# Cross-attention and FFN on one core: rows turned by TensorE in place of DMA transposes, the last output projection made by rows, and a new written order of all steps

## The chip, the cores and the metric

The kernel runs on one core of a Trainium2 chip. The metric is the device time of one execution in microseconds (us), lower is better. The runs shown are executions of the same program; one further execution was taken with the hardware profiler.

## The reference, cut to what matters

Eight elements of 112 tokens with 512 channels attend to contexts of 375 rows with 256 channels, in 16 heads of 128 channels; then an FFN of 512 x 2048 x 512 whose operands are rounded to 127 levels a side, by rows for the tokens and over the whole matrix for the weights.

```python
def attn(h, c):                       # h = layernorm(x)
    q = rmsnorm((h @ Wq).reshape(B, Sq, H, D), gq)
    k = rmsnorm((c @ Wk).reshape(B, Skv, H, D), gk)
    v = (c @ Wv).reshape(B, Skv, H, D)
    p = softmax(einsum('bqhd,bkhd->bhqk', q, k) / sqrt(D))
    return einsum('bhqk,bkhd->bqhd', p, v).reshape(B, Sq, H * D) @ Wo

def ffn(x):                           # x = layernorm(x)
    X1_q, sX1 = quantize_rowwise(x)   # round(x * 127 / absmax of the row), and absmax
    W1_q, sW1 = quantize_global(W1)
    X2 = gelu(X1_q @ W1_q.T * (sX1 * sW1 / 127**2) + B1)
    X2_q, sX2 = quantize_rowwise(X2)
    W2_q, sW2 = quantize_global(W2)
    return X2_q @ W2_q.T * (sX2 * sW2 / 127**2) + B2

x = x + attn(layernorm(x), ctx)
x = x + ffn(layernorm(x))
```

## The kernel before, in words

**Tiling.** Elements go in four pairs p = 0 to 3 (`BP` = 2, `NPAIR` = 4, `TP` = 224 tokens of a pair), heads in four groups of four (`HG`, `NG`). A group of a pair has a number G = 4p + g (0 to 15, `NGG` = 16), and a group of one element a number u = 2G + i (0 to 31). Attention matmuls are fp32; each shows as two matmul instructions in the profile, while transposes show as one. The FFN matmuls are bf16, for the rounded values are whole numbers to 127.

**Spare rows.** A tile has 128 rows and an element 112 tokens. The 16 spare rows of elements 1 to 7 carry element 0 (for the queries, element 7) in seven parts, so the FFN runs over seven elements, 1 to 7.

**Steps.** Each piece of work is a small function registered as a step with a short name; a word such as `w0.26` in the written order plays step `w0` at place 26. The order is written by hand as four scripts, one for each pair; negative places reach back into the pair before. TensorE, VectorE, ScalarE and the SP queue each run their instructions strictly in that order (`in_written_order`). `after(...)` only asserts that a step was played earlier; semaphores follow from the data and the buffers. All plain DMAs are issued from SP.

**Steps of attention for one u or G.** `k0..k2` keys (`pkk`), `kc`, `kq`, `kr`, `ka..kd`, `kn` their normalization, `kt`, `ks`, `kf` the turning of keys by 32x32 blocks on VectorE and two trips through DRAM (`kz`, `kd`, `kT`); `Q`, `S`, `qt`, `qs`, `qf`, `G` the same for queries; `s0..s3` scores (`sc`); `x`, `e`, `iv`, `n` softmax; `z`, `ps`, `pf` the turning of probabilities (`pz`, `pd`, `pT`), for the first and the last u by TensorE instead (`pt`, `pk`); `w0`, `w1` the probabilities times the context (`pu`, kept by `v` as `wc`); `o`, `u` times Wv (`po`, kept as `oT`); `p`, `a` times Wo (`pw`), with channels on partitions, added on VectorE into `aT`. For the last group, G = 15, `O`, `U`, `P`, `A` do this for each element alone.

**From attention to FFN.** Pairs 0 to 2: `rz`, `rs`, `rf`, `rn` turn `aT` back to rows by blocks and DRAM and add it to the tokens (`x2`). The last pair: `ra` turns `aT` on TensorE (L965) after the last `A`, and `rb` adds it. Then `st` (statistics), `fa`, `fb`, `fc`, `fd` (the root), `fi` (normalize and row maximum), `fq` (round to bf16 `xq`).

**FFN of one element.** The rows must be turned before each of the two products. Elements 6 and 7: `ti` on TensorE (L1052), kept by `tj` (L1060, VectorE); hidden rows by `tp0..tp3`, kept by `tk0..tk3` (L1060, ScalarE or VectorE). Elements 1 to 5: one DMA transpose each, `td` for the input rows and `te` for the hidden ones (`send_rows`, L1073). `h0..h3` is the first product (L1080), `i0..i3` scale and bias (L1089), `ge` (or `g0..g3`) gelu with a load of the activation table before and after, `lm` (or `mx`, `es`) the row maximum, `qh` (or `qp`, `qq`) rounding, `y0`, `y1` (or `Y0..Y3`) the second product (L1159), `yo`, `yd` the residual and the output.

**PSUM.** All matmul tiles but the scores rotate through four buffers (`mm_tile`, pool `ps_mm`): a new tile waits until the one four before has been read. Scores have four of their own.

Of the kernel before, what the change touches and what calls it, by code (L numbers as in the profile page):

```python
# [30 lines left out]
def xattn_ffn_kernel(  # L31
# [870 lines left out]
    def project(G, lo, n, c0):  # L902
        if n == TP:
            after(("u0", G), ("u1", G))
        else:
            after((f"U{lo // S}", G))
        pw = T["pw", G, lo, c0] = mm_tile(f"pw_{G}_{c0}_{lo}")
        for c in range(c0, c0 + NW // n):
            for h in range(HG):
                nc.tensor.matmul(  # L910
                    pw[:, (c - c0) * n : (c - c0 + 1) * n], T["wo", G][:, h, c * P : (c + 1) * P],
                    T["oT", G][:, h, lo : lo + n], start=(h == 0), stop=(h == HG - 1),
                )
# [13 lines left out]

    for n in range(2):
        step(f"o{n}", NG, values, 0, TP, 2 * n)
        step(f"u{n}", NG, value_keep, 0, TP, 2 * n)  # L930
        step(f"p{n}", NG, project, 0, TP, 2 * n)
        step(f"a{n}", NG, project_add, 0, TP, 2 * n)
        step(f"O{n}", NG, values, n * S, S, 0)
        step(f"U{n}", NG, value_keep, n * S, S, 0)
        step(f"P{n}", NG, project, n * S, S, 0)
        step(f"A{n}", NG, project_add, n * S, S, 0)
# [19 lines left out]
    def turn_sum(b):  # L956

        p, i = divmod(b, BP)
        if p == NPAIR - 1:
            after((f"A{i}", NGG - 1))  # L960
        else:
            after(("a0", p * NG + NG - 1), ("a1", p * NG + NG - 1))
# [50 lines left out]
    def stats(b):  # L1013
        after(("rb" if b >= B - BP else "rn", b), ("zf", b))
# [4 lines left out]
    def row_absmax(src, name):  # L1019
        m = small.tile([P, 1], F32, tag="rowmax", name=name)  # L1020
# [8 lines left out]
    def norm_in(b):  # L1029
        after(("fd", b))  # L1030
        xn = T["xn2", b] = ffn.tile([P, C], F32, tag="y", name=f"xn2_{b}")
        nc.vector.tensor_scalar(xn, x2_of(b), T["mv2", b][:, 0:1], T["rstd2", b], ALU.subtract, ALU.mult)
        T["m1", b] = row_absmax(xn, f"m1_{b}")
        T["d1", b] = dequant_scale(T["m1", b], absw1, f"d1_{b}")
# [6 lines left out]
    def quantize_in(b):  # L1041
        quantize_rows(home("xq", b, [P, C], BF16), T["xn2", b], quant_scale(T["m1", b], P))
# [27 lines left out]
    def send_rows(b, what):  # L1070

        to = home(what + "T", b, [P, KC if what == "xq" else KF, P], BF16)
        nc.sync.dma_start_transpose(out=to, in_=T[what, b])  # L1073

# [9 lines left out]
    def hidden_keep(b, n):  # L1084
        after(("lb", 0))
# [27 lines left out]
    def pieces_scale(b):  # L1113
        after(*[(f"mx{n}", b) for n in range(NF4)])
        m = small.tile([P, 1], F32, tag="rowmax", name=f"m2_{b}")
# [23 lines left out]
    def turn_piece(b, n):  # L1139
        after((f"qq{n}", b))  # L1140
# [46 lines left out]
    step("fi", BP, norm_in)  # L1187
    step("fq", BP, quantize_in)
# [3 lines left out]
    step("td", BP, send_rows, "xq")  # L1192
    step("te", BP, send_rows, "hq")
# [13 lines left out]
    for n in range(2):  # L1207
# [7 lines left out]
        cz.0 lk.0 cz.1 lf.0 lf.1 lx.0 l7.0 gl.0 lc.1 kh.0 jl.0 lk.1 lq.0 jl.3 jl.6 kh.1 xs.1 xs.0 xa.1  # L1215
        xc.1 xs.7 ct0.0 kc0.0 xa.0 xb.7 k0.1 kc1.0 xb.1 xd.1 xc.0 xm.1 xa.7 kq0.0 xc.7 k1.1 kr0.0 kq1.0
        kc2.0 xb.0 xd.0 kc0.1 kr1.0 ck0.0 ct0.1 xm.0 kq2.0 xt.1 xd.7 kc1.1 cz.2 xt.0 kr2.0 ck0.1 k2.1
        kb.0 ka.0 xm.7 ke.0 kq0.1 kd.0 xk.0 kn2.0 xt.7 xk.1 gm.0 kn0.0 kv2.0 xk.7 jm.0 kc2.1 xl.0 kv0.0
        kq1.1 lq.1 k0.2 kw0.0 kw2.0 kn1.0 xy.0 xy.1 kr0.1 kv1.0 kr1.1 kq2.1 Q0.0 kr2.1 kb.1 ka.1 jm.3
        kc0.2 ke.1 Q1.0 qt0.0 kw1.0 qs0.0 lx.1 kd.1 jl.1 kn1.1 qv0.0 kn0.1 S0.0 kt0.1 k1.2 kq0.2 kn2.1  # L1220
        S1.0 kt2.1 qw0.0 sa.0 sb.0 kc1.2 kt1.1 k2.2 kq1.2 ks.1 qt1.0 sc.0 qx0.0 sd.0 qv1.0 kr0.2 kc2.2
        k0.3 kr1.2 kq2.2 qs1.0 kr2.2 lc.2 s2.0 lv.0 kb.2 s7.0 ct1.0 qw1.0 lk.2 s1.0 qx1.0 ck1.0 s3.0
        jm.1 kc0.3 s0.0 ka.2 kq0.3 k1.3 ke.2 x0.0 kf.1 k2.3 kc1.3 ly.0 x1.0 e0.0 jl.7 Q0.1 kd.2 e2.0
        kn2.2 e3.0 kn0.2 e1.0 iv.0 xs.3 n0.0 kc2.3 kn1.2 pt0.0 n2.0 k0.4 qt0.1 S0.1 xs.2 qs0.1 n3.0
        kt0.2 kq1.3 pt2.0 pt3.0 pk0.0 kt1.2 n1.0 s1.1 kt2.2 pk2.0 ct1.1 cb0.2 kc0.4 ks.2 s0.1 cb1.2
        pt1.0 kr0.3 s3.1 kr1.3 kq0.4 k1.4 xa.3 pk3.0 jl.2 ck1.1 kr0.4 kq2.3 pk1.0 k2.4 x0.1 xb.3 s2.1
        e0.1 kr2.3 Q1.1 kc1.4 kb.3 ka.3 kc2.4 ke.3 kq1.4 kd.3 kq2.4 kn0.3 xc.3 kf.2 e1.1 x1.1 qf0.1 k0.5
        lq.2 kt0.3 lk.3 e2.1 kn2.3 e3.1 w0.0 xd.3 iv.1 kr1.4 n0.1 n2.1 z0.1 xa.2 qt1.1 w1.0 n1.1 n3.1
        kn1.3 qs1.1 S1.1 z1.1 z3.1 k1.5 z2.1 sb.1 G0.1 xm.3 ps.1 v0.0 kt1.3 s1.2 kr2.4 s2.2 kb.4 ka.4
        kt2.3 ke.4 s0.2 sa.1 xc.2 ks.3 sc.1 s3.2 kc0.5 sd.1 kc1.5 x0.2 k2.5 kq0.5 x1.2 e0.2 lo.0 Q0.2  # L1230
        kq1.5 kr0.5 kc2.5 e3.2 kd.4 kn0.4 kq2.5 e2.2 kn1.4 v1.0 qt0.2 S0.2 k0.6 pf.1 qf1.1 e1.2 cs.2
        Q1.2 kt0.4 qs0.2 kn2.4 kt2.4 iv.2 k1.6 kt1.4 n1.2 kf.3 n0.2 kr1.5 ks.4 n3.2 xb.2 z0.2 S1.2 xd.2
        jm.2 kc0.6 n2.2 lq.3 w0.1 xm.2 G1.1 sa.2 kc1.6 k2.6 qt1.2 qf0.2 z3.2 w1.1 ja.0 z1.2 sb.2 z2.2
        kr2.5 s1.3 v1.1 cz.3 lc.3 v0.1 s2.3 ps.2 ka.5 o0.0 sc.2 js.0 s0.3 kb.5 u0.0 js.1 qs1.2 ke.5 k0.7
        kc2.6 kq1.6 kd.5 s3.3 kn0.5 s7.1 o1.0 x0.3 lk.4 kf.4 kt0.5 e0.3 Q0.3 x1.3 kq0.6 e1.3 kn2.5 u1.0
        G0.2 kr0.6 e2.3 kn1.5 k1.7 kt2.5 pf.2 kt1.5 kr1.6 kc0.7 ks.5 e3.3 k2.7 iv.3 cb0.3 n1.3 qt0.3
        n2.3 Q1.3 lv.1 kc1.7 cb1.3 qs0.3 sd.2 kc2.7 js.2 n0.3 kq2.6 kq0.7 kr2.6 n3.3 qf1.2 s3.4 kr0.7
        ka.6 S0.3 s1.4 z0.3 s0.4 ke.6 z3.3 kq1.7 z1.3 p0.0 kq2.7 z2.3 S1.3 x0.4 ps.3 jr.0 s2.4 sa.3 jr.1
        lk.5 p1.0 kf.5 qt1.3 x1.4 G1.2 qs1.3 w0.2 e0.4 kr2.7 e1.4 kb.6 kd.6 kr1.7 qf0.3 k0.8 pf.3 a0.0
        ka.7 e3.4 lo.1 a1.0 e2.4 sb.3 az.0 k1.8 iv.4 kb.7 n0.4 kn2.6 v0.2 kn0.6 sc.3 kt0.6 z0.4 s3.5  # L1240
        s2.5 xu.2 s1.5 kn1.6 G0.3 s0.5 n3.4 kt2.6 qf1.3 w1.2 n2.4 xv.2 z3.4 kt1.6 z2.4 kc0.8 x0.5 ke.7
        w0.3 ks.6 n1.4 kc1.8 sd.3 kq0.8 jr.2 v1.2 w1.3 e0.5 cs.3 z1.4 G1.3 k2.8 v1.3 v0.3 xu.3 xw.2 jl.4
        x1.5 o0.1 ps.4 kd.7 e2.5 kn0.7 o1.1 kc2.8 kn2.7 kq1.8 kf.6 kn1.7 lq.4 k0.9 js.3 xv.3 xk.2 k1.9
        u0.1 kr0.8 u1.1 xy.2 kr1.8 e3.5 cf.2 kt0.7 s7.2 e1.5 k2.9 kq2.8 iv.5 kt1.7 n2.5 kt2.7 p1.1 n3.5
        cz.4 kr2.8 kc0.9 kq0.9 jm.4 kc1.9 n0.5 pf.4 kc2.9 n1.5 z0.5 ka.8 kq1.9 z3.5 z2.5 kb.8 z1.5 s1.6
        kr0.9 ps.5 s0.6 jr.3 kq2.9 s3.6 p0.1 x0.6 kr2.9 e0.6 kr1.9 ke.8 e1.6 xw.3 jm.6 s2.6 lx.2 Q0.4
        s7.3 ks.7 kd.8 kb.9 a1.1 a0.1 w0.4 qt0.4 S0.4 kn0.8 kn2.8 x1.6 k0.10 pf.5 kn1.8 e2.6 k1.10 xk.3
        ka.9 xy.3 v0.4 xs.4 jl.5 w1.4 qs0.4 xb.4 xa.4 k2.10 kt0.8 lv.2 kt1.8 kf.7 lk.6 kt2.8 kc0.10 ks.8
        xc.4 w0.5 e3.6 xd.4 ke.9 iv.6 kc1.10 kd.9 xs.5 lo.2 w1.5 v0.5 jm.7 kc2.10 v1.4 kq0.10 co0.2 Q1.4
        qf0.4 xa.5 n3.6 n0.6 n2.6 z0.6 v1.5 z3.6 n1.6 jm.5 kq1.10 o1.2 S1.4 s0.7 z1.6 kn0.9 s1.7 kn2.9  # L1250
        s2.7 qt1.4 o0.2 kn1.9 qs1.4 z2.6 k0.11 x0.7 kt0.9 e0.7 ps.6 s3.7 kt2.9 co1.2 k1.11 u0.2 x1.7
        u1.2 kr0.10 lq.5 k2.11 e3.7 kf.8 ja.1 kt1.9 s7.4 kr1.10 kc0.11 p0.2 kq2.10 sb.4 G0.4 kr2.10
        kc1.11 sa.4 e1.7 sc.4 e2.7 p1.2 sd.4 a0.2 ka.10 pf.6 ke.10 kc2.11 kb.10 ks.9 kd.10 kq1.11 iv.7
        n0.7 n2.7 z0.7 k0.12 n3.7 xm.4 kq0.11 z3.7 n1.7 z2.7 Q0.5 a1.2 kr0.11 kr1.11 z1.7 kq2.11 kn1.10
        ps.7 kn2.10
    """, 0)
    play("""
        s0.0 js.-3 s2.0 s3.0 cf.1 k1.4 qt0.1 lc.2 qf1.0 kn0.2 qs0.1 w0.-2 kt0.2 kt1.2 lv.-1 s1.0 kt2.2
        kr2.3 kc0.4 pf.-1 xc.3 xb.3 w1.-2 js.-4 ka.3 kf.1 v0.-2 ks.2 S0.1 x0.0 kq0.4 k2.4 kc1.4 v1.-2
        js.-1 Q1.1 kc2.4 kb.3 ke.3 js.-2 co0.1 G1.0 kq2.4 kd.3 kn2.3 kr0.4 S1.1 lq.2 lk.3 x1.0 kq1.4  # L1260
        qf0.1 co1.1 w0.-1 lo.-1 qt1.1 e0.0 sb.1 e1.0 kr1.4 kn0.3 w1.-1 v0.-1 kr2.4 e3.0 e2.0 jr.-4 iv.0
        kn1.3 s3.1 s0.1 s1.1 kt0.3 n0.0 s2.1 xd.3 n2.0 z0.0 v1.-1 k0.5 kt1.3 n1.0 n3.0 z2.0 sa.1 z1.0
        k1.5 z3.0 kt2.3 ps.0 x1.1 o0.-1 kc0.5 x0.1 o1.-1 u0.-1 qs1.1 sc.1 ka.4 kc1.5 Q0.2 u1.-1 e0.1
        kf.2 G0.1 ks.3 e2.1 e3.1 e1.1 p0.-1 kq0.5 iv.1 s7.1 n0.1 kq1.5 z0.1 pf.0 n3.1 kr0.5 ke.4 S0.2
        z3.1 p1.-1 n1.1 kb.4 n2.1 z1.1 z2.1 qt0.2 ps.1 kd.4 k2.5 xm.3 cb0.2 kr1.5 qf1.1 s3.2 jr.-3 qs0.2
        k0.6 a0.-1 kn0.4 cb1.2 lv.0 sd.1 w0.0 a1.-1 kn1.4 kn2.4 s0.2 kt0.4 pf.1 s1.2 kt2.4 G1.1 s2.2
# [135 lines left out]
```

## Time and profile before

| | us |
|---|---|
| median of 3 runs | 720.77 |
| lowest, highest | 720.21, 721.2 |
| the profiled execution | 720.28 |
| its span in the profile | 718.5 |
| TensorE busy | 702.7 |
| VectorE busy | 537.3 |
| ScalarE busy | 433.6 |
| DMA, hardware queue, share of 16 engines | 85.1% |
| mean granted TensorE clock | 0.999 |

The span runs from the first to the last event of the profiled execution; the 1.8 us beside it lie around it. A group of instructions is shown as line, engine, operation, output<-input, shape and count, then busy time, mean ns of one, and the idle time before them with what ended it. A row of waits is engine, line, what it waited for, us in total, times, longest. A row of the timeline is start, duration, engine, line, operation and count, with the wait before it in brackets. A row of the chain is start, duration, engine, tile, line and count.

### The profile page before, as it was taken

The page shows a single profiled execution, that of the slowest core. Times are in us where ns is not written, and L with a number is a line of the kernel's source. Part 1 is how long each engine was busy: PE and PEld are TensorE (multiplying, and loading weights), DVE is VectorE, ACT ScalarE, POOL GpSimd, SP SyncE. Part 2 cuts the span into 40 slices and gives each one's busy share as a digit, 9 for nine tenths or more (in the row PEclk, how much of TensorE's full clock was granted, in tenths as well). Part 3 has the DMA queues.
Part 4 walks back from the last instruction along what each step waited for, and adds up shares of the span by engine and source line. Part 5 has one row for each costly group of instructions (what it writes and reads, how often), then busy time and mean ns, then how long its engine had stood idle before and what let it go on. Part 6 is the DMA issues. An engine that isn't in the chain of part 4 may idle for free.

```text
span 718.5 us, 8555 instructions
## 1 busy us (share of the span) xinstructions
PE 702.7 (98%) x2398; PEld 413.3 (58%) x2410; DVE 537.3 (75%) x1234; ACT 433.6 (60%) x1129; POOL 2.4 (0%) x10
## 2 busy tenths in 40 slices
PE   9999999999999999999999999999999999999976
PEld 4444456655657564745656465564657455667742
DVE  6997888887876677747857787868774898964395
ACT  5677576636475756556466556666755566627325
POOL 0000000000000000000000000000000000000000
PEclk9999999999999999999999999999999999999999
DMA  8799999989988999999898989999999889998201
GB/s 304 266 280 298 294 298 282 301 268 290 282 308 244 293 285 313 269 275 310 227 289 286 295 265 287 287 240 305 292 257 291 237 256 272 259 290 282 34 1 44
DMA packets 131246, 187.85 MB, mean 261 GB/s; under 512 B 34864, under 2 KB 90800, under 8 KB 130560
## 3 DMA queue, kind: packets, MB, share of 16 engines
q1 hardware_dynamic: 131200, 187.32, 85.1%
q8 instruction: 19, 0.31, 0.2%
q14 instruction: 27, 0.22, 0.1%
HBM read 124.55 MB, written 59.45 MB: 256 GB/s over the span
## 4 chain that ended last, share of the span: by engine, by line
PE 85%; DVE 5%; ACT 4%; DMA 3%; SPq 1%; issue 1%; POOL 0%; ACTq 0%; DVEq 0%; POOLq 0%
PE pkk L650 19%; PE pu L860 17%; PE pw L910 13%; PE pq L532 12%; PE sc L758 10%; PE po L887 6%; PE py L1159 2%; PE ph L1080 2%; DMA pT<-pd 1%; PE pkk L660 1%; DMA kT<-kd 1%; ACT probs L780 1%; DMA qr<-q 1%; DMA qss<-s 1%; ACT qsq L547 1%
## 5 line engine op out<-in xcount | busy, mean ns | idle before, releaser
L650 PE MATMUL pkk<-wk,cT 128*128 128x512 f32 x372 | 171.8, 593 | 0.3 <-DVE hid L1089 0.3
L860 PE MATMUL pu<-pT,c 128*128 128x448 f32 (+1 forms) x384 | 152.3, 540 | 1.0 <-DMA pT<-pd 1.0
L860 PEld LDWEIGHTS pu<-pT,c 128*128 128x128 f32 (+1 forms) x384 | 72.5, 190 | 71.3 <-issue 61.7
L780 ACT ACTIVATE probs<-sc,bias,rq 112x375 f32<-112x375 f32 x128 | 84.1, 663 | 47.8 <-DVE bias L773 47.8
L650 PEld LDWEIGHTS pkk<-wk,cT 128*128 128x128 f32 x372 | 70.0, 190 | 72.3 <-issue 60.9
L910 PEld LDWEIGHTS pw<-oT,wo 128*128 128x128 f32 x544 | 98.2, 190 | 9.8 <-issue 6.5
L910 PE MATMUL pw<-oT,wo 128*128 128x224 f32 (+1 forms) x544 | 101.8, 343 | 0.6 <-ACT oT L897 0.6
L532 PE MATMUL pq<-wq,xnT 128*128 128x512 f32 x224 | 100.2, 592 | 0.0
L758 PE MATMUL sc<-kT,qT 128*112 128x384 f32 x256 | 92.4, 486 | 0.3 <-DMA kT<-kd 0.2
L670 ACT COPY kk<-pkk 128x512 f32<-128x512 f32 x96 | 55.2, 580 | 58.6 <-DVE kz L698 25.6
L797 DVE STREAM_TRANSPOSE pz<-probs 128x384 f32<-128x384 f32 x120 | 63.7, 558 | 21.1 <-ACT probs L791 18.2
L791 ACT ACTIVATE probs<-probs,inv 112x375 f32<-112x375 f32 x128 | 72.1, 605 | 8.9 <-DVE inv L788 8.9
L771 DVE TENSOR_REDUCE top<-sc 112x1 f32<-112x375 f32 x128 | 63.8, 535 | 18.0 <-PE sc L758 17.5
L681 DVE TENSOR_REDUCE kss<-ksq 128x4 f32<-128x512 f32 x96 | 63.1, 668 | 14.0 <-ACT ksq L675 14.0
L532 PEld LDWEIGHTS pq<-wq,xnT 128*128 128x128 f32 x224 | 42.4, 190 | 49.6 <-issue 46.5
L758 PEld LDWEIGHTS sc<-kT,qT 128*112 128x112 f32 x256 | 44.7, 177 | 38.9 <-issue 16.7
L675 ACT ACTIVATE ksq<-kk 128x512 f32<-128x512 f32 x96 | 59.5, 628 | 6.4 <-DVE kss L681 6.0
L688 DVE TENSOR_TENSOR kk<-kk,rk 128x512 f32<-128x512 f32 x96 | 62.9, 675 | 0.5
L698 DVE STREAM_TRANSPOSE kz<-kk 128x512 f32<-128x512 f32 x93 | 62.3, 690 | 0.9 <-issue 0.4
L871 ACT COPY wc<-pu 128x448 f32<-128x448 f32 x64 | 33.5, 531 | 36.6 <-PE pu L860 36.6
L887 PEld LDWEIGHTS po<-wc,wv 128*128 128x128 f32 x272 | 49.1, 190 | 8.0 <-issue 4.1
L887 PE MATMUL po<-wc,wv 128*128 128x224 f32 (+1 forms) x272 | 53.1, 344 | 0.0
(122 smaller groups left out, 590.8 us busy)
## 6 DMA issues: line engine op xcount, KB each, us to landing
kd<-kz SPq DMA_DIRECT2D x124, 192.0 KB, 4.0
kT<-kd SPq DMA_DIRECT2D x31, 768.0 KB, 6.4
pT<-pd SPq DMA_DIRECT2D x30, 672.0 KB, 6.1
pd<-pz SPq DMA_DIRECT2D x90, 192.0 KB, 4.4
wq<-in_wq SPq DMA_DIRECT2D x16, 1024.0 KB, 7.7
wo<-in_wo SPq DMA_DIRECT2D x16, 1024.0 KB, 7.8
wv<-in_wv SPq DMA_DIRECT2D x16, 512.0 KB, 5.8
wk<-in_wk SPq DMA_DIRECT2D x15, 512.0 KB, 6.2
```

The costliest lines, as they stand in the source:

```text
L532: nc.tensor.matmul(pq[:, :GW], T["xnT", p][:, k, i * P : (i + 1) * P], T["wq", G][:, k, :], start=(k == 0), stop=(k == KC - 1),)
L650: nc.tensor.matmul(pk[:, :GW], T["cT", batch_of(u)][:, k, j * P : (j + 1) * P], T["wk", u // BP][:, k, :], start=(k == 0), stop=(k == KCC ...
L681: nc.vector.tensor_reduce(T["kss", u][:, j, :], T.pop(("ksq", u, j)).rearrange("p (h d) -> p h d", d=D), AX.X, ALU.add)
L688: nc.vector.tensor_tensor(kv, kv, T["rk", u][:, j, :].unsqueeze(2).to_broadcast([P, HG, D]), ALU.mult)
L758: nc.tensor.matmul(sc[:S, :SKP].rearrange("p (j i r) -> p j i r", j=NJ, r=BK), T["qT", G, i][:, h, :], T["kT", u][:, :, :, h, :].rearrange ...
L771: nc.vector.tensor_reduce(top[:, h : h + 1], T["sc", u, h0 + h][:S, :SK], AX.X, ALU.max, negate=True)
L780: nc.scalar.activation(p_bufs[h][:S, :SK], T["sc", u, h][:S, :SK], AF.Exp, bias=T["bias", u, h0][:, h - h0 : h - h0 + 1], scale=rq_of(u, h ...
L791: nc.scalar.mul(p_bufs[h][:S, :SK], p_bufs[h][:S, :SK], T["inv", u][:, h : h + 1])
L797: nc.vector.transpose(T["pz", u][:, :, :, :, h, :].rearrange("p a f j q -> p j a f q"), p_bufs[h].rearrange("p (j a r) -> p j a r", j=NJ, ...
L860: nc.tensor.matmul(pu[:, : HG * S], T["c", b][: ROWS[j], j, k * P : (k + 1) * P], T["pT", u][: ROWS[j], :, j, :, :].rearrange("p f h q -> ...
L887: nc.tensor.matmul(po[:, (h - h0) * n : (h - h0 + 1) * n], T["wv", G][:, k, h * D : (h + 1) * D], T["wc", G][:, k, h, :, :].rearrange("p b ...
L910: nc.tensor.matmul(pw[:, (c - c0) * n : (c - c0 + 1) * n], T["wo", G][:, h, c * P : (c + 1) * P], T["oT", G][:, h, lo : lo + n], start=(h ...
```

## The change

1. `send_rows` and its steps `td`, `te` go. Elements 1 to 5 are turned as elements 6 and 7 were: `ti`, `tj`, `tp0..tp3`, `tk0..tk3`. For them `tp` asks for the whole row's rounding (`qh1`).
2. For the last group `P`, `A` go. `R` (`project_rows`) multiplies with the values as the stationary operand, so its result has tokens on partitions, and `rc` (`rows_add`) adds it to `x2`. `ra` turns the sum of the groups before (up to G = 14) and no longer follows the last group.
3. `fi` only subtracts the mean and takes the maximum; the root enters in a new step `fe`, through the scale `d1`. Rounding needs no root, since a row's scale cancels in it.
4. All four scripts are new orders of the same steps.

The built program has 100 matmuls and 100 weight loads more for the turns (TensorE), 16 + 16 projection matmuls of 112 columns fewer and 8 of 512 columns more, 20 copies more on ScalarE, and 10 DMA transposes fewer on SP.

```diff
     def project(G, lo, n, c0):
-        if n == TP:
-            after(("u0", G), ("u1", G))
-        else:
-            after((f"U{lo // S}", G))
+        after(("u0", G), ("u1", G))
...
+    def project_rows(i):
+
+        after((f"U{i}", NGG - 1))
+        pr = T["pr", i] = mm_tile(f"pr_{i}")
+        for h in range(HG):
+            nc.tensor.matmul(
+                pr[:S, :], T["oT", NGG - 1][:, h, i * S : (i + 1) * S], T["wo", NGG - 1][:, h, :],
+                start=(h == 0), stop=(h == HG - 1),
+            )
+
+    def rows_add(i):
+        x2 = T["x2", NPAIR - 1][:S, i, :]
+        after(("rb", B - BP + i))
+        nc.vector.tensor_tensor(x2, x2, T.pop(("pr", i))[:S, :], ALU.add)
+
+    step("R", BP, project_rows)
+    step("rc", BP, rows_add)
...
-        step(f"P{n}", NG, project, n * S, S, 0)
-        step(f"A{n}", NG, project_add, n * S, S, 0)
...
     def turn_sum(b):
 
         p, i = divmod(b, BP)
-        if p == NPAIR - 1:
-            after((f"A{i}", NGG - 1))
-        else:
-            after(("a0", p * NG + NG - 1), ("a1", p * NG + NG - 1))
+        after(("a0", NGG - 2), ("a1", NGG - 2))
...
     def stats(b):
-        after(("rb" if b >= B - BP else "rn", b), ("zf", b))
+        after(("rn", b) if b < B - BP else ("rc", b - B + BP), ("zf", b))
...
     def norm_in(b):
-        after(("fd", b))
+
+
+        after(("st", b))
         xn = T["xn2", b] = ffn.tile([P, C], F32, tag="y", name=f"xn2_{b}")
-        nc.vector.tensor_scalar(xn, x2_of(b), T["mv2", b][:, 0:1], T["rstd2", b], ALU.subtract, ALU.mult)
+        nc.vector.tensor_scalar(xn, x2_of(b), T["mv2", b][:, 0:1], None, ALU.subtract)
         T["m1", b] = row_absmax(xn, f"m1_{b}")
-        T["d1", b] = dequant_scale(T["m1", b], absw1, f"d1_{b}")
+
+    def scale_in(b):
+        after(("fi", b), ("fd", b))
+        m = small.tile([P, 1], F32, tag="rowmax2", name=f"m1r_{b}")
+        nc.vector.tensor_tensor(m, T["m1", b], T["rstd2", b], ALU.mult)
+        T["d1", b] = dequant_scale(m, absw1, f"d1_{b}")
...
-    def send_rows(b, what):
-
-        to = home(what + "T", b, [P, KC if what == "xq" else KF, P], BF16)
-        nc.sync.dma_start_transpose(out=to, in_=T[what, b])
-
...
     def turn_piece(b, n):
-        after((f"qq{n}", b))
+        after((f"qq{n}", b) if b >= B - BP else ("qh1", b))
         turn_rows("hq", b, n * (NW // P), NW // P)
```

The end of the last script, from the first weighing of element 6's last group, before and after (in each, TensorE's steps alone):

```
before: w0.30 pt3.31 pt0.31 w1.30 pt2.31 pt1.31 O0.15 w0.31 P0.15 w1.31 ra.6 O1.15 P1.15 ti.6 ra.7
        h0.6 h1.6 h2.6 h3.6 ti.7 y0.5 h0.7 h1.7 y1.5 h2.7 h3.7 tp0.6 tp3.6 tp1.6 Y0.6 tp2.6 Y1.6 Y2.6
        Y3.6 tp0.7 tp3.7 tp2.7 tp1.7 Y0.7 Y1.7 Y2.7 Y3.7
after:  w0.30 w1.30 pt1.31 pt0.31 pt3.31 O0.15 ra.6 pt2.31 R.0 w0.31 w1.31 tp2.5 tp3.5 tp0.5 O1.15
        ra.7 ti.6 R.1 h0.6 h1.6 tp1.5 h2.6 y0.5 h3.6 ti.7 y1.5 h0.7 h1.7 tp0.6 h2.7 h3.7 tp1.6 tp2.6
        Y0.6 Y1.6 tp3.6 Y2.6 Y3.6 tp0.7 tp1.7 Y0.7 tp2.7 Y1.7 tp3.7 Y2.7 Y3.7
```

(Here a step's place is its number counted over all pairs: the u, the element or the group; `R.0` and `R.1` are elements 6 and 7.)

## The prediction

> **What bounds the kernel now.** I read the engine rows and the slices of the page first, then the chain that ended last, then TensorE's waits, then the timeline of the last 55 us.
>
> ```profile
> span 718.5 us, 8555 instructions
> PE 702.7 (98%) x2398; PEld 413.3 (58%) x2410; DVE 537.3 (75%) x1234; ACT 433.6 (60%) x1129; POOL 2.4 (0%) x10
> PE   9999999999999999999999999999999999999976
> PEclk9999999999999999999999999999999999999999
> DMA  8799999989988999999898989999999889998201
> PE 85%; DVE 5%; ACT 4%; DMA 3%; SPq 1%; issue 1%; POOL 0%; ACTq 0%; DVEq 0%; POOLq 0%
> ```
>
> TensorE is busy in every slice but the last two, at the full granted clock, and is 85% of the chain. But ends of matmuls are modelled, so I test "busy" by pace. The chain's rows give the pace of each shape when it runs dense:
>
> ```profile
> 211.34 3.43 PE pkk L650 x8
> 119.39 2.58 PE sc L758 x8
> 121.97 6.77 PE pu L860 x18
> 214.77 3.03 PE po L887 x16
> 628.62 3.45 PE py L1159 x16
> ```
>
> That is 0.429, 0.322, 0.376, 0.189 and 0.216 us an instruction. Times the counts: 608 fp32 ones of 512 columns 261; 256 scores 82; 384 weighings 144; 720 of 224 columns 136; 96 of 112 columns at 0.112 11; 224 bf16 ones of 512 columns 48 (the page holds 212, a few records are missing); all transposes 10. Sum 693 us. The first key matmul starts at 5.2 and the last matmul ends at 714.3, so in 709 us TensorE loses 16 us. Where?
>
> ```profile
> PE pxq L1052 <- DVE xq L1039: 3.2, 1, 3.2
> PE phq L1052 <- ACT hq L1137: 1.6, 3, 0.8
> PE pu L860 <- DMA pT<-pd: 1.0, 1, 1.0
> PE py L1159 <- ACT hqT L1060: 0.9, 1, 0.9
> ```
>
> The waits are few. From the timeline, 9.5 us are lost after 663.5 (50.8 us there, 41.3 us of matmuls), some 3 before 50 us, and under 4 in the 613 us between. The middle runs at TensorE's pace, so work put on TensorE there is paid in full, and work taken off other engines or queues there can give back under 4 us.
>
> **The change part by part.** *Rows turned on TensorE.* Five elements (1 to 5) lose two DMA transposes each and get 4 + 16 transposes of 128x128 bf16: 100. The order view agrees: in it 100 matmuls and 100 weight loads are new at this line. How dear one is, the last two elements show:
>
> ```profile
> 702.75 0.62 PE L1052 MATMUL phq<-ident_h,hq 128*128 128x128 bf16 x8 [0.57 <-ACT hq L1137]
> L1052 PE MATMUL phq<-ident_h,hq 128*128 128x128 bf16 x32 | 2.8, 220 | 1.7 <-ACT hq L1137 1.6
> L1060 ACT COPY hqT<-phq 128x512 bf16<-128x512 bf16 x6 | 3.2, 570 | 0.0
> ```
>
> One lasts 220 ns, but eight that follow each other take 0.62 us: (0.62 - 0.22) / 7 = 0.057 us each. So 100 x 0.056 = 5.6 us. Here the Trainium skill ("TensorE: Matmul & The Clock Gate", Part 4: PE-mode transpose) speaks against the change: about 275 ns in a kernel and 390 alone for this shape, and such work does not count as busy for the clock. By it the sum would be 27 to 39 us. The 220 ns row agrees with it as a latency; the pace does not, because transposes overlap, and here they stand between dense fp32 matmuls that hold the clock. I take 5.6.
>
> After each group an fp32 matmul follows, whose weights load under one 0.056 us transpose only. The 112-column projections run at 0.112 us with 128-column weights, and 112-column transposes with 112-column weights at 0.096, so a full fp32 load seems to need some 0.11 us: up to 0.056 more for each of 25 groups, 0 to 1.4; no row shows a bf16 transpose before an fp32 load undisturbed. I take the middle, 0.7.
>
> *Copies and small work.* 7 products of 0.16 us (maximum times root) and 5 copies of 416 ns on VectorE (75% busy), and 20 copies of 570 ns on ScalarE (11.4 us, it is 60% busy) lie under TensorE's work. The copies hold PSUM slots: 344 tiles rotate through the four slots instead of 319. A new tile waits for the copy of the one four before. In matmul time between the two, the tightest places outside start and tail were 2.4 and 2.6 us before (p1.14, o0.6, p0.12), and are 1.7 to 2.2 now (y0.2, p0.6, tp0.3, tp3.3 with the tiles behind). A copy of 0.57 us that finds its engine free needs far less; one queued behind two or three others does not. 0 to 5 us, taken 0.
>
> *DMA transposes gone.*
>
> ```profile
> L1073 SPq DMA_TRANSPOSE xqT<-xq x5: 1194/1207/1461, 308.4 to 607.1; - x5
> L1073 SPq DMA_TRANSPOSE hqT<-hq x5: 1323/3762/5465, 349.8 to 669.4; - x5
> SPq L1073 <- DVE pT L834: 10.6, 1, 10.6
> ```
>
> Ten issues held the SP queue 24 us (the columns are shortest, median and longest in ns), and SP waited 28 us more at that line (the longest wait is shown) with the loads behind it. In bytes they are 3.2 of 187 MB. No TensorE wait names one: y follows h by 30 us of matmuls, keys lead scores by 28 or more. So the gain is bounded by the under 4 us of the middle; taken 0, for in the new order every load, send and fetch stands elsewhere in the one SP queue too and can be late in its turn: the same steps, 10 issues fewer, the lead of keys over scores at least 30 us of matmuls as before, that of scores over weighing at least 23 where a transfer lies between (21 before).
>
> *Last projection by rows.* Before, 2 x 32 instructions of 112 columns: 7.2 us. Now 2 x 8 of 512 columns: 6.9. -0.3.
>
> *Tail.* Count from the first weighing of element 6's last group (663.5 before). 41.3 us of matmuls remain there before, 41.9 now (16 turns of element 5 at 0.9, projection -0.3). Walk through the new order with durations of the old trace. ScalarE's gelu of element 5 with two table loads ends at 4.8; weights kept at 5.9; O0 6.0 to 7.75; the turn of the sums and one of the probabilities fill the wait for the copy of O0, which cost 0.8 us in the old O1; R0 8.6 to 12; weighing of element 7 to 16.5; three turned pieces to 17.2; O1 to 19.05; R1 19.9 to 23.35. VectorE: add 24.25, statistics 25.15, two biases of the hidden rows 26.7, subtract and maximum 28.2, quantization 29.5. So TensorE turns element 7 at 29.6 instead of 31.2. But its copy stands on VectorE behind two biases, a maximum, the root and the scale, and lands at 33.8; so h0 of element 7 starts at 33.9 (33.1 before). Then y's add 0.75 and two maxima 1.4, scale of element 6 at 36.5 (35.2), first turned piece at 38.0 (38.3), scale of element 7 at 45.0 (43.5), last matmul at 51.5 (50.8). What was saved is spent in VectorE's queue: the split normalization takes the root off the chain but adds a 0.16 us product. Tail +0.7, of which 0.6 is matmul work counted above: stall change +0.1, say -3 to +3.
>
> *Start.* Tokens before keys, contexts earlier: the first queries at 23.9 - or 22.5 if x lands as before; then kv without its 0.6 us wait. 0, +-1.5.
>
> Sum: 5.6 + 0.7 - 0.3 + 0.1 = 6.1. The profiled execution (720.28, span 718.5, 1.8 around it) would become 726.4; the median of runs is 0.5 above it, 720.8, so 726.9.
>
> **The rivals.** *More stalls than matmuls:* each of 25 turn groups waits for an operand or a slot, 0.2 to 0.4 us, as VectorE at 75% and a fuller ScalarE fall behind on an in-order TensorE. 25 x 0.3 = 7.5: 734. For: slots are tighter; DMA transposes kept rows off TensorE's queue. Against: the old kernel is as tight in places and shows no such wait in the middle.
>
> *Faster:* the SP queue is freed, so the transfer waits of the middle vanish (say -3), and the tail stalls shrink. It decides when TensorE's lost time falls from 16 to under 8.5 us. For: in the old chain TensorE waits for transfers between 505 and 576 (qss, qr, kT, pT), just where SP issues transposes. Against: it must come mostly from the tail, and my walk finds none there. -3 and -5 there, +6.1: 718.9.
>
> *A wash:* half of it, -5: 722.
>
> *Turning is dear:* 0.275 us each, +27: 748. It would be so if turning serialized between fp32 matmuls; against it stands the pace row.
>
> **How the numbers follow.** Main 0.63, more stalls 0.19, faster 0.09, a wash 0.06, dear turning 0.03. A measurement of this kernel tells about 0.2% (1.4 us) from no change. The main case holds 724 to 730; the range goes to 721.5 below (part of the wash) and 732 above (half of the stall case). Faster 0.09, same 0.06, slower 0.85.
>
> **What would show it.** 140 bf16 transposes, TensorE busy about 708 with the middle dense, and no transpose issues on SP. Groups at L1052 with 8.5 us busy in all; if it is over 20, turning was dear. Waits of TensorE on ACT or DVE copies in the middle over 4 us mean the stall rival. In the tail, h0 of element 7 should start by the wait for its xqT copy on VectorE; a last stretch of under 46 us from that weighing would make me wrong and favour the faster case.

## Result, and the profile after

Slower by 1.1%. The changed kernel takes 728.41 us (median of 4 runs, 727.05 to 732.18) beside 720.99 for the kernel before in the same runs (720.21 to 721.59): a ratio of 1.0112, with a 95% interval of 1.0072 to 1.0152. Its profiled execution took 727.59 us, with a span of 725.8.

The page of the kernel after: span, engine rows, the slices of TensorE and of its clock, the shares of the chain.

```profile
span 725.8 us, 8699 instructions
PE 709.5 (98%) x2462; PEld 413.3 (57%) x2462; DVE 539.0 (74%) x1246; ACT 444.1 (61%) x1149; POOL 2.4 (0%) x10
PE   8999999999999999999999999999999999999986
PEclk9999999999999999999999999999999999999999
PE 89%; DVE 4%; ACT 3%; DMA 3%; issue 1%; SPq 0%; ACTq 0%
```

TensorE is as dense as before, at the full clock. Its share of the chain is 89% after 85%, but that share is no steady figure: a second profile of the same kernel (run 9) has 75%. VectorE's and ScalarE's busy time grew by 2 and 10 us without becoming the bound. TensorE's waits (total, times, longest), without the 1.2 us of the warming matmuls ahead of the first keys, which the kernel before has too, and 0.6 us more in the tail:

```profile
PE phq L1069 <- ACT hq L1149: 2.3, 3, 1.8
PE ph L1092 <- DVE xqT L1077: 1.5, 1, 1.5
PE pxn L398 <- ACT ksq L675: 1.0, 1, 1.0
PE pu L860 <- ACT qsq L547: 0.7, 1, 0.7
PE pkk L650 <- ACT oT L897: 0.6, 1, 0.6
PE pq L532 <- ACT wc L871: 0.6, 1, 0.6
PE pu L860 <- DVE hid L1101: 0.6, 1, 0.6
PE pxq L1069 <- ACT qsq L547: 0.5, 1, 0.5
```

The first two belong to the tail; before, waits of 3.2, 1.6 and 0.9 us stood there. The third is in the start. The other five, 3.0 us together, are new in the middle, and none is for a transfer: each ends, by the profile, when VectorE or ScalarE has read a PSUM tile.

To split the 7.3 us of span I compare the matmuls' starts with the dense pace of their shape (the paces of the prediction), in three stretches: to 54 us, from there to the first weighing of element 6's last group, and the tail from there to the last matmul. Single matmul records that are missing are filled in; a sum is good to about 0.5 us.

| kernel | lost in the start | lost in the middle | tail, whole time |
|---|---|---|---|
| before | 2.9 | 3.9 | 51.0 |
| after | 4.5 | 6.6 | 48.9 |

TensorE's work grew from about 692.7 to 698.2 us. So: +5.5 of work, +1.6 lost in the start, +2.7 in the middle, and in the tail 2.1 less though 0.6 of the work was added there, so 2.7 less lost. 5.5 + 1.6 + 2.7 - 2.7 = 7.1, beside 7.3 in the span.

What one turn costs, from the rows of L1069 (shortest, median and longest in ns):

```profile
L1069 PE MATMUL phq<-ident_h,hq x112: 217/219/230, 350.8 to 719.7; 128*128 128x128 bf16 x112
L1069 PE MATMUL pxq<-ident_h,xq x28: 217/219/230, 305.3 to 701.7; 128*128 128x128 bf16 x28
```

All 140 are there. 219 ns is what one lasts; their starts inside a group are 55 or 56 ns apart, and in 16 of the 18 places where an fp32 matmul follows a group, it also starts 55 to 56 ns after the last turn (in the other two 169 and 181).

The tail on TensorE's timeline, some rows of it:

```profile
688.76 0.83 PE L1069 MATMUL phq<-ident_h,hq 128*128 128x128 bf16 x12
692.20 3.69 PE L930 MATMUL pr<-wo,oT 128*112 128x512 f32 x8
701.52 0.40 PE L1069 MATMUL pxq<-ident_h,xq 128*128 128x128 bf16 x4 [0.23 <-DVE xq L1055]
705.13 1.90 PE L1092 MATMUL ph<-wff,xqT 128*128 128x512 bf16 x8 [1.49 <-DVE xqT L1077]
708.82 0.40 PE L1069 MATMUL phq<-ident_h,hq 128*128 128x128 bf16 x4 [1.80 <-ACT hq L1149]
719.80 1.89 PE L1171 MATMUL py<-wff,hqT 128*128 128x512 bf16 x8
```

Twelve turns take 0.83 us between fp32 matmuls. Element 7 is turned at 701.5, its first product waits 1.49 us for VectorE's copy, and the first turned piece of element 6's hidden rows waits 1.80 us for its rounding.

### The profile page after: what moved, and what is told of

Read it like the earlier page. It is cut to its first block, busy times and chain, and to the rows that moved or that the text cites. A ratio compares the mean times of both kernels' runs of the same rounds, so it can differ in the third digit from the quotient of the medians.

```text
span 725.8 us, 8699 instructions
## 1 busy us (share of the span) xinstructions
PE 709.5 (98%) x2462; PEld 413.3 (57%) x2462; DVE 539.0 (74%) x1246; ACT 444.1 (61%) x1149; POOL 2.4 (0%) x10
## 4 chain that ended last, share of the span: by engine, by line
PE 89%; DVE 4%; ACT 3%; DMA 3%; issue 1%; SPq 0%; ACTq 0%
PE pkk L650 21%; PE pu L860 18%; PE pw L907 13%; PE pq L532 12%; PE sc L758 11%; PE po L887 7%; PE py L1171 2%; PE ph L1092 2%; DMA rt<-rd 1%; ACT qsq L547 1%; PE pr L930 1%; DMA x<-in_x 1%; PE phq L1069 1%; DVE bn L171 0%; DVE hid L1101 0%
## 5 line engine op out<-in xcount | busy, mean ns | idle before, releaser
L758 PE MATMUL sc<-kT,qT 128*112 128x384 f32 x256 | 95.1, 488 | 0.7 <-ACT qT L626 0.3
L907 PEld LDWEIGHTS pw<-oT,wo 128*128 128x128 f32 x480 | 90.5, 190 | 8.4 <-issue 5.2
L907 PE MATMUL pw<-oT,wo 128*128 128x224 f32 x480 | 95.2, 353 | 0.0
L532 PEld LDWEIGHTS pq<-wq,xnT 128*128 128x128 f32 x224 | 42.3, 190 | 49.4 <-issue 45.0
```

The source lines that it names most:

```text
L532: nc.tensor.matmul(pq[:, :GW], T["xnT", p][:, k, i * P : (i + 1) * P], T["wq", G][:, k, :], start=(k == 0), stop=(k == KC - 1),)
L758: nc.tensor.matmul(sc[:S, :SKP].rearrange("p (j i r) -> p j i r", j=NJ, r=BK), T["qT", G, i][:, h, :], T["kT", u][:, :, :, h, :].rearrange ...
L907: nc.tensor.matmul(pw[:, (c - c0) * n : (c - c0 + 1) * n], T["wo", G][:, h, c * P : (c + 1) * P], T["oT", G][:, h, lo : lo + n], start=(h ...
```

## Experiments

Each is timed beside the kernel before. That kernel's medians were 722.21 us beside runs 1 to 4, 721.60 beside runs 5 to 8 and 722.98 beside runs 9 to 12 (11, 25 and 16 executions), so I compare ratios between these groups. The stretches of all of them, measured as above:

| kernel | ratio to before, 95% interval | start | middle | tail |
|---|---|---|---|---|
| 1 old order, turns on TensorE | 1.0116 [1.0095, 1.0138] | 2.6 | 8.4 | 52.9 |
| 2 new order, DMA transposes | 1.0168 [1.0138, 1.0198] | 4.2 | 15.3 | 48.7 |
| 3 after, turns twice | 1.0147 [1.0123, 1.0172] | 4.5 | 6.5 | 49.4 |
| 4 after, old projection | 1.0125 [1.0100, 1.0149] | 6.4 | 6.2 | 51.0 |
| 5 old order, new tail | 0.9967 [0.9951, 0.9983] | 2.8 | 4.3 | 48.7 |
| 6 as 5, one copy on ScalarE | 0.9970 [0.9952, 0.9988] | 2.9 | 4.0 | 48.6 |
| 7 as 2, transposes late | 1.0156 [1.0122, 1.0190] | 6.3 | 18.1 | 48.7 |
| 8 after, root first | 1.0124 [1.0101, 1.0148] | 5.6 | 11.4 | 48.9 |
| 9 after again | 1.0098 [1.0066, 1.0131] | 4.5 | 8.0 | 48.9 |
| 10 after, first keys first | 1.0067 [1.0041, 1.0093] | 4.3 | 7.1 | 48.9 |
| 11 after, sums later | 1.0071 [1.0046, 1.0096] | 4.7 | 5.2 | 48.9 |
| 12 both | 1.0059 [1.0038, 1.0080] | 3.8 | 6.7 | 48.9 |

The tail is steady to 0.3 us among kernels that share it. The middle moved by 1.4 us between two profiles of one kernel (after and run 9), so a step of that size is shown only where the wait itself is seen to go. Every kernel with the new order lost 3.8 us or more in the start, every one with the old order 2.6 to 2.9.

**1. The old order, with the turns on TensorE.** `td` and `te` of elements 1 to 5 become `ti`, `tj`, `tp0..3`, `tk0..3`, put 4 to 13 us of matmuls ahead of their use; everything else is the kernel before.

```diff
-        after((f"qq{n}", b))
+        after((f"qq{n}", b) if b >= B - BP else ("qh1", b))
...
-... pf.5 k1.9 td.-1 kd.8 kn1.8 ... xw.3 ks.7 w0.5 ...
+... pf.5 k1.9 kd.8 kn1.8 ... xw.3 ks.7 ti.-1 w0.5 tj.-1 ...
```

> The old order and the old projection; only the ten DMA transposes become 100 transposes on TensorE, each group placed some 4 to 13 us of matmuls ahead of its product. Matmul time alone (0.056 us each): +5.6 us, 726.4, with no new waits in the middle. Dear turning[...]: +22 to +27, 743 or more. Slots (the turned tiles make the waits of the middle): +5.6 and some 3 us of waits of TensorE on copies between 50 and 660 us, 729.5. The new order alone is to blame for the loss: no change, 721.

Measured 730.51 us: as slow as the whole change. Work rose to about 698 as in after, and the middle lost 4.5 us more than before. Where, its timeline of TensorE shows:

```profile
469.94 0.39 PE L1052 MATMUL phq<-ident_h,hq 128*128 128x128 bf16 x4
471.00 1.78 PE L887 MATMUL po<-wc,wv 128*128 128x224 f32 x8 [0.68 <-ACT hqT L1060]
472.61 0.39 PE L1052 MATMUL phq<-ident_h,hq 128*128 128x128 bf16 x4
473.68 1.98 PE L650 MATMUL pkk<-wk,cT 128*128 128x512 f32 x4 [0.68 <-ACT hqT L1060]
```

Here TensorE waits out the copy of the piece that it has just turned. ScalarE is not late: it had stood idle for 2.14 us when the first of these pieces ended (470.33), and began the copy at once (470.36, 0.59 us long). In the built program the next matmul tile has the very PSUM buffer of the turned piece, in both places. In four places the matmul behind a turned piece starts late, by 3.3 us together. So turns alone cost their matmuls and here nearly as much again, most of it right behind the turned pieces. In the tail 1.0 us more is lost than before, where the granted clock was 0.50 from 704.75 to 708.16 us (last section). And TensorE's waits for transfers in the middle stayed without any DMA transpose: 1.1 us (0.5 for `pT`, 0.6 for `kT`) after 1.2. No hidden gain lay there.

**2. The new order, with DMA transposes.** After, but `td` stands right behind `fq` and `te` right behind `qh1` for elements 1 to 5.

```diff
+    def send_rows(b, what):
+
+        to = home(what + "T", b, [P, KC if what == "xq" else KF, P], BF16)
+        nc.sync.dma_start_transpose(out=to, in_=T[what, b])
+
...
-... kc0.9 fq.-1 o1.1 ... s0.6 z3.5 ti.-1 p1.1 tj.-1 ...
+... kc0.9 fq.-1 td.-1 o1.1 ... s0.6 z3.5 p1.1 ...
```

> The changed kernel with its new order, but elements 1 to 5 turned by DMA transposes again, issued right behind the rounding. Matmul time: -5.6 us, 722.8, and the waits in the middle near 324, 416, 430 and 454 us stay, for the order makes them. Slots: those waits go with the 25 tiles, -8.5, 720. DMA transposes held the SP queue back: transfers come late and the gain is under 4 us, 724.5 or more.

Measured 733.27 us. The 5.6 us of turns are gone (work 692.5) and 9 us more are lost in the middle. TensorE's waits, four of them:

```profile
PE pu L860 <- DMA pT<-pd: 5.0, 3, 2.5
PE pu L860 <- ACT qsq L547: 1.0, 1, 1.0
PE pq L532 <- ACT wc L871: 0.6, 1, 0.6
PE pu L860 <- DVE hid L1106: 0.6, 1, 0.6
```

The last three are also among the five of after: the new order makes them without the turned tiles. The first is not in after. Where part of it comes from, the SP queue shows:

```profile
530.14 4.36 SPq L1090 DMA_TRANSPOSE hqT<-hq  x1
534.60 0.53 SPq L817 DMA_DIRECT2D pT<-pd  x1
```

The issue of the transpose holds the queue for 4.36 us, and the fetch of turned probabilities goes out behind it; TensorE waits for it from 537.44 to 539.68. In after that fetch goes out at 528.03, right behind the fetch of queries, which here stands right ahead of the transpose. SP's longest wait is another matter:

```profile
SPq L1090 <- DVE xn L1043: 21.9, 1, 21.9
```

It is at the last transpose, issued at 690.04, with only sends of the output behind it (the next at 709.28), so it holds up nothing that TensorE waits for. The longest of TensorE's waits for `pT`, in the timeline:

```profile
363.69 6.47 PE L860 MATMUL pu<-pT,c 128*128 128x448 f32 x12 [2.46 <-DMA pT<-pd]
```

and the stretches around it (bounds; PE, PEld, DVE, ACT, POOL busy; granted clock; DMA share; GB/s):

```profile
360.00:363.69 3.69, 1.23 (x3) 0.19 (x1) 3.59 (x11) 0.00 (x0) 0.00 (x0) 1.00 0.96 352
363.69:367.20 3.51, 3.51 (x6) 1.66 (x7) 1.22 (x4) 0.00 (x0) 0.00 (x0) 0.57 1.05 379
```

After the wait the clock is halved for 3.4 us: six weighings fill 3.51 us, where dense ones take 2.3.

**3. Every added turn twice.**

```diff
-        for k in range(k0, k0 + n):
+        for k in [k for k in range(k0, k0 + n) for _ in range(2 if b < B - BP else 1)]:
```

> The changed kernel with each of the 100 transposes of elements 1 to 5 issued twice into the same place. Matmul time: +5.6 us, 734.0. Dear turning: +22 to +27, over 750. If turning hides in gaps of TensorE: under +2.

Measured 732.63 us. Its span of 731.0 is 5.2 and 4.6 us above the two profiles of after (725.8, 726.4): 100 more turns cost 46 to 52 ns each. Single waits moved (one of 1.7 us at 63.8 is new, those on `qsq` are gone), but the sums lost in start and middle are those of after. By the ratios of medians they cost 2.5 to 3.5 us, with intervals that overlap those of after. At the lasting 219 ns they would have cost 22 us.

**4. The projection as before, the rest as after.** `P`, `A` return for the last group, then `ra`, `rb`; the `ra` of element 7 stands one step later, behind element 6's first hidden product.

```diff
-        after(("a0", NGG - 2), ("a1", NGG - 2))
+        after((f"A{i}", NGG - 1))
...
-... ra.0 U0.3 pt2.7 rb.0 R.-6 pk2.7 ... w0.7 rc.-6 qh1.-1 ...
+... U0.3 pt2.7 P0.3 pk2.7 ... w0.7 A0.3 qh1.-1 ra.0 rb.0 ...
```

> The changed kernel with the last group projected by channels again (32 instructions of 112 columns an element, added into the sum, then turned and added to the tokens). Row projection shortens the tail: +2.5 us (the tail lost 7.0 us where it lost 9.5 before) and +0.3 of matmuls, 731. Rival, the tail is bound by VectorE's queue and its order: +0.3 to +1, 729.

Measured 731.16 us. The tail is 51.0 us instead of 48.9, so the projection by rows is worth 2.1 us, 0.3 of it matmuls. All of it is there when element 7 is turned, 30.9 us after the first weighing instead of 28.8. Each of the old pieces waits for the values' copy and takes longer; compare the row of 692.20 above with

```profile
694.26 3.83 PE L910 MATMUL pw<-oT,wo 128*128 128x112 f32 x32 [0.33 <-ACT oT L897]
```

The heads' sum must still be turned (`ra`) and added (`rb`) behind them. The rest of its excess lies in the start (6.4, with 3.4 us at half the clock there), which the edit does not touch; in the whole time its interval overlaps that of after.

**5. The old order and DMA transposes up to the tail, then the new tail.** All four scripts of the kernel before up to `w0.30`, with `fe` behind each `fi`; behind it the order of after, with `te` of element 5 kept in place of its turned pieces.

```diff
-... w0.6 iv.7 n3.7 n2.7 n0.7 pt3.7 pt0.7 w1.6 pk0.7 n1.7 pk3.7 v0.6 ...
+... iv.7 n1.7 n3.7 n0.7 w0.6 w1.6 v0.6 pt1.7 v1.6 pt0.7 n2.7 pt3.7 pk0.7 O0.3 pk3.7 pk1.7 ra.0 ...
```

> The old order and its DMA transposes up to the first weighing of element 6's last group; from there the new order with the projection by rows and the split normalization, without turned pieces of element 5, whose hidden rows keep their DMA transpose. If the tail's gain (lost time 9.5 to 7.0 us) belongs to the tail alone and the turns and the new order before it are what costs: -2.5 to -3 us against the kernel before, 718.3. If the tail gained only because the turned pieces of element 5 or the new order ahead of it filled its gaps: no change.

Measured 719.23 us, faster than both kernels: 0.9967 of the kernel before. Start and middle stay as before (2.8, 4.3), the tail is that of after. Page rows:

```profile
span 715.9 us, 8464 instructions
PE 700.7 (98%) x2350; PEld 408.4 (57%) x2362; DVE 537.1 (75%) x1241; ACT 434.3 (61%) x1129; POOL 2.4 (0%) x10
```

So the part of the change that helps is the tail, and it needs no turns on TensorE.

**6. As 5, with element 7's copy on ScalarE,** right behind its turn, for the 1.5 us wait that stands in VectorE's queue.

```diff
-        keep_rows("xq", b, 0, KC, nc.vector.tensor_copy)
+        keep_rows("xq", b, 0, KC, nc.scalar.copy if b == B - 1 else nc.vector.tensor_copy)
```

> The kernel of the run before, and element 7's copy of the turned rows on ScalarE right behind the turn, where it stood on VectorE behind biases, maxima and the root. TensorE's wait of 1.65 us before h0 of element 7 goes. If VectorE's chain to the row maximum of element 6 then sets the rest: the wait moves to the first turned piece of element 6, and only the 0.4 us of the copy are won, 717.9. If the wait was TensorE's own: -1.5, 716.8.

Measured 718.85 us, the same as run 5. The wait went and came back behind the next: in run 5 the copy's wait was 1.5 and the first turned piece's 1.8; now there is one,

```profile
PE phq L1069 <- DVE hid L1148: 3.1, 1, 3.1
```

and behind it the granted clock falls, as the windows show:

```profile
695.50:699.00 3.50, 0.37 (x5) 0.15 (x4) 3.40 (x11) 0.85 (x2) 0.00 (x0) 1.00 0.24 75
699.00:702.50 3.50, 3.37 (x19) 1.85 (x19) 3.31 (x6) 3.43 (x7) 0.00 (x0) 0.62 0.00 0
```

VectorE is busy for 3.40 of the 3.5 us of the wait: the tail hangs on its chain for element 6's hidden rows, and work moved off it elsewhere only joins two waits.

**7. As 2, with the transposes as late as leaves 9 to 11 us of matmuls,** on the reading that the wait of 21.9 us had held the fetches up.

```diff
-... z0.4 kr2.8 k0.9 u1.1 ...
+... z0.4 kr2.8 td.-1 k0.9 u1.1 ...
```

> As the run with the new order and DMA transposes, but each transpose stands later in the SP queue where there is room: as late as leaves 9 us of matmuls before h0 and 11 before y0. In the earlier run one stood 21.9 us in SP's queue waiting for its rows and the fetches of probabilities behind it came late. If that placement made the loss: the waits on pT go, and -5.6 from the turns remains, 722 to 724. If the new order has no room for transposes in the SP queue wherever they stand: over 728.

Measured 733.20 us (726.88 to 735.73; the profile is of the slowest). It did not help:

```profile
PE pu L860 <- DMA pT<-pd: 6.2, 3, 3.0
```

The reading was wrong: SP's longest wait, 23.6 us, is again at the last transpose (694.39), where it delays nothing. What delays fetches is in part the issue of transposes, and the pair of run 2 is still there: a transpose at 529.97 that holds the queue for 4.74 us, the fetch at 534.80, a wait of 2.44 us. Runs 2 and 7 are not the only places that transposes could have in this order. What they show is that neither placement beat the 5.6 us of turns; the interval of run 2 lies above that of run 9, that of run 7 overlaps it.

**8. The root before the normalization again,** `fi` multiplying as before and the scale without the product; `fa` to `fd` move ahead of `fi`.

```diff
-        nc.vector.tensor_scalar(xn, x2_of(b), T["mv2", b][:, 0:1], None, ALU.subtract)
+        nc.vector.tensor_scalar(xn, x2_of(b), T["mv2", b][:, 0:1], T["rstd2", b], ALU.subtract, ALU.mult)
```

> The changed kernel, but rows are normalized with the root again before their maximum (fi after fd), the scale without the product. If the split normalization is what shortens the tail: +1 to +2 us, 730. If the row projection is it: +0 to +0.5, 728.7.

Measured 730.04 us, its interval overlapping that of after. The tail is 48.9 in both: the split is worth nothing there. Its profile lost 11.4 us in the middle against 6.6 and 8.0; one profile cannot say how much of that is the split.

**9. After again.** Kernel unchanged.

> The changed kernel itself, beside the three below. 728.4 as before; spread among its executions goes with the granted clock (725.3 to 729.2 us of span at 1.000 to 0.998).

Measured 729.22 us, ratio 1.0098; span 726.4. Its spread does not go with the clock, as was expected: the slowest execution, 733.31 us, had a granted clock of 1.000. It is the yardstick for the next three.

**10. The first keys ahead of the tokens' turns,** `xt.0` and `xt.1` behind `k1.1`.

```diff
-... kc2.0 xt.0 kq1.0 xt.1 kc0.1 kr1.0 k1.1 lx.1 ...
+... kc2.0 kq1.0 kc0.1 kr1.0 k1.1 xt.0 xt.1 lx.1 ...
```

> The changed kernel, but the two turns of tokens (xt) stand behind the second key block of element 1 instead of ahead of it. If their 1.1 and 0.7 us of waits at 12 and 14 us are lost time of the start: -1.5 to -1.8 us against the changed kernel. If the start is bound by what comes later (key norms, loads): 0 to -0.5.

Measured 727.53 us, 1.7 below run 9 in the medians, but the intervals overlap and the start lost 4.3 instead of 4.5: the waits at 12 to 14 us were only moved, to the second keys (on their contexts) and later turns. Inconclusive; what the start's 1.6 us hang on was not found.

**11. The fetched sums added later,** for elements 2 and 4, so that VectorE does not wait for them in front of the keys' sums.

```diff
-... kc0.6 kq2.5 rn.-2 lo.0 st.-2 iv.2 ... w0.1 kr2.5 kq0.6 ...
+... kc0.6 kq2.5 lo.0 iv.2 ... w0.1 kr2.5 rn.-2 st.-2 kq0.6 ...
```

The reason, in the timeline of after:

```profile
412.71 0.69 DVE L1006 TENSOR_TENSOR x<-x,rt 112x512 f32<-112x512 f32 x1 [1.29 <-DMA rt<-rd]
414.33 1.25 DVE L681 TENSOR_REDUCE kss<-ksq 128x4 f32<-128x512 f32 x2
415.08 0.63 ACT L675 ACTIVATE ksq<-kk 128x512 f32<-128x512 f32 x1 [2.93 <-DVE kss L681]
417.71 3.65 PE L860 MATMUL pu<-pT,c 128*128 128x448 f32 x9 [0.74 <-ACT qsq L547]
```

VectorE waits for a fetched sum, so the keys' sums come late, so ScalarE idles 2.93 us before its next squares and reads the query tile late, so the weighing that wants its slot waits.

> The changed kernel, but for elements 2 and 4 the add of the fetched sums (rn) and the statistics stand a few words later in VectorE's order (behind two key sums, or behind a score maximum), and element 4's turn a few words later on TensorE. If VectorE's waits for the fetched sums (1.3 and 2.8 us) are what made ScalarE late, and ScalarE's late reading of query tiles what held TensorE at 416 and 585 us: these waits of 0.9 and 0.7 us go, -1.5 us. If the 25 turned tiles in the four slots make them: no change.

Measured 727.86 us; span 724.4 beside 726.4 in run 9. What VectorE waits for these sums, in run 9 and here (us, times), each from the tile's view:

```profile
  DMA rt<-rd: 3.2, 2
```

```profile
  DMA rt<-rd: 1.0, 1
```

and the wait of TensorE on `qsq`, 1.3 us in run 9, is gone from its list:

```profile
PE pu L860 <- ACT qsq L547: 1.3, 1, 1.3
```

The middle lost 5.2 instead of 8.0, though the medians differ by 1.4 with overlapping intervals. The other three waits of the middle, of 0.6 us each, stay.

**12. Both edits.**

> Both edits of the two runs before. If the terms add: -3 us against the changed kernel, 725.4, with 5.3 us of work, and less lost time than the kernel before left.

Measured 726.95 us, 0.0039 under run 9's ratio, which is 2.8 us of the 3 expected, though the intervals overlap. The wait on `qsq` stays away, but, by the profile, TensorE waits 1.1 us for weights (`wo`) and 0.7 us on VectorE ahead of a first FFN product instead. This is the changed kernel with the two repairs found, and its whole interval lies above the kernel before: neither of them, nor both, won back the added matmuls.

## Why the prediction was right, and where its sizes were off

Direction and size were right: 726.9 predicted, 728.41 measured. The signs named for it came: 140 turns, TensorE busy 709.5 us, no transposes on SP, and under 4 us of waits on copies in the middle (3.0). Term by term, predicted against measured:

- **100 turns at 0.056 us, 5.6.** Right: starts 55 to 56 ns apart, +5.5 of work, and in run 3 the span grew by 4.6 to 5.2 for 100 more. The figures weighed there (the Trainium skill, "TensorE: Matmul & The Clock Gate", Part 4: 390 ns alone, 275 ns in one kernel) are times of one transpose; 219 ns is that here, and dense code pays the pace. With 140 of them the granted clock stayed at 1.000. "Dear turning" is refuted.
- **The fp32 weight load behind a group, 0.7.** Zero: that interval is 55 to 56 ns too. The trace puts the start of such a load 54 ns ahead of its matmul; how it finds room there is not shown.
- **Projection, -0.3.** Right: 3.69 against 3.83 us for each element.
- **Copies and slots, 0 (0 to 5).** This is the term that was mis-sized: +2.7 in the middle. The step at fault is "A new tile waits for the copy of the one four before", which the description of the kernel says too. In the built program the four buffers do not go round in turn: of 341 tiles that take over a buffer, 161 follow the tile four before, the others one from one to seven before. In two places it is the tile just before, and both are among the five waits:

```profile
431.21 0.53 ACT L897 COPY oT<-po 128x448 f32<-128x448 f32 x1 [3.40 <-PE po L887]
431.79 2.41 PE L650 MATMUL pkk<-wk,cT 128*128 128x512 f32 x5 [0.62 <-ACT oT L897]
454.92 0.53 ACT L871 COPY wc<-pu 128x448 f32<-128x448 f32 x1 [7.10 <-PE pu L860]
455.51 2.84 PE L532 MATMUL pq<-wq,xnT 128*128 128x512 f32 x6 [0.62 <-ACT wc L871]
```

  ScalarE is free there, waiting for the tile (3.40 and 7.10 us), and TensorE waits out the whole copy; "a copy of 0.57 us that finds its engine free needs far less" does not help with no other matmul between. In two more the reader is late in its queue: `qsq` (run 11), and `hid`, which reads the tile three before and stands behind a turn of queries that waited 3.29 us for its matmuls. The fifth, a turn at 586.33, starts 0.05 us after its own rows were rounded, so it need not be a wait for a buffer. Three of the five (`hid`, `qsq`, `wc`) stand in run 2 without the turned tiles: for these the new order is enough. The term is a third of what "more stalls" asked for, at five places instead of 25.
- **DMA transposes gone, 0.** Right for the old order (run 1). In after the 1.2 us of waits for transfers did go, though run 9 has 0.5 again. In the new order transposes, as placed in runs 2 and 7, cost no less than the turns, but that is a price of that order.
- **Tail, +0.1 lost.** Wrong by 2.8: -2.7. The order of events was as walked, with the wait for element 7's copy behind VectorE's queue at 705.1 and no shorter chain by the split root (run 8). But the walk summed durations for the new order and set them beside a measured tail for the old one. It ran long from the start: counted from that weighing, R0 began at 7.96 us (walked 8.6), element 7's copy ended at 32.3 (33.8), the first turned piece came at 36.1 (38.0), the end at 48.9 (51.5). That excess of 2.6 us is the size of the gain that it missed; whether a walk of the old order would have run as long was not tried. Run 4 names most of the gain: the projection by rows, 2.1 us, for which the walk had booked only 0.3. The other 0.9 us come from the rest of the new tail and were not taken apart.
- **Start, 0 +-1.5.** +1.6, and it comes with the new order. Tokens' turns lose 1.1 and 0.7 us at 12 to 14 us by their normalization and slots, but run 10, which moved them, did not repair it, so this cause stays open.

The wrong terms nearly cancel: -0.7 (weight load) + 2.7 (slots) - 2.8 (tail) + 1.6 (start) = +0.8 on the predicted 6.1, and the span grew by 7.3. That the sum came so close is luck; the pace of a turn is not. The "faster" rival looked for its gain in transfers; about half of what it asked of the tail was there, but mostly by the projection, and the middle and the start gave it back.

## What to carry to other kernels

When one engine is dense, price added work by its start-to-start pace in a dense group, and take it as paid in full; transfers removed from a queue that nobody waits for pay nothing back. Where tiles share a few buffers, read from the built program which tile had the buffer before, and put other matmuls between the two. Compare a walk through a new order with the same walk through the old one and not with its measurement: here the walk was off by as much as the effect. Then take a bundle apart: here the tail of the change alone, on the old order, beat both versions by 0.3% or more.

## What the runs showed of the hardware

A single wait of TensorE can cost more than itself. After waits of 3.24 us (run 1), 2.46 us (run 2), 3.13 us (run 6) and 3.02 us (run 7), the granted clock fell to half for 3.41 us; in run 2 that cost 1.2 us more. But the kernel before had the very wait of run 1 and kept its clock:

```profile
694.65 0.40 PE L1052 MATMUL pxq<-ident_h,xq 128*128 128x128 bf16 x4 [3.24 <-DVE xq L1039]
```

The clock records of the traces show the difference. Between two changes of the clock there is always a whole number of stretches of 3.413 us (in run 7: 3, 1, 189, 1 and 19), so changes fall on a fixed grid. The grid stretches ahead of the four falls held 2.3 to 3.2 us without a matmul. The wait of the kernel before is cut by a grid line into 1.8 and 1.4 us, and in the fourteen traces no stretch that kept the clock held more than 1.97 us. So it counts where a wait falls, and not only how long it is. In the start, between turns of tokens, the clock fell after stretches with only 1.7 us without a matmul (runs 4 and 7); why is open. The Trainium skill ("TensorE: Matmul & The Clock Gate", Part 1) says that activity is judged in windows of about 3.4 us that run on freely; the grid agrees. That a wait of 2.46 us can suffice is the measurement's.

The issue of a DMA transpose holds the queue that issues it, 1.2 to 2.7 us for input rows and 1.3 to 5.6 us for hidden ones (runs 2 and 7), and what stands behind it goes out that much later. In run 2 a fetch behind an issue of 4.36 us left TensorE waiting for 2.24 us. Where only sends of the output stood behind one, even 19 to 24 us of waiting ahead of it cost nothing (runs 2, 5 and 7).
